# Later LSTM steps by Strassen's seven products, and x through common buffers and DRAM

## The chip, the cores and the metric

The kernel runs on one core of a Trainium2 chip. The metric is the device time of one execution in microseconds (us). The kernel before took 2199.53 us, the median of three runs (2198.49 to 2202.52). The profile shows a further execution, timed at 2196.78 us; its span from the first to the last instruction is 2195.0 us, at a granted TensorE clock of 0.998.

## The reference, cut to what matters

Input x has 128 batches of 64 rows with 256 features, that is 8192 rows. Four layers follow each other, each of the form x = x + f(relu(layernorm(x))):

```python
# layer 0: two graph convolutions with the 64x64 matrix adj, then four LSTMs
h = relu(adj @ (h @ Wg0 + bg0)); h = relu(adj @ (h @ Wg1 + bg1))
for p in range(1, 5):                  # windows of p rows
    nw = 64 // p
    wins = h[:, :nw * p].reshape(128 * nw, p, 256)
    last = lstm(Wih[p-1], Whh[p-1], wins)   # p steps, last hidden state
    h[:, p-1 : nw*p : p] = last
# one LSTM step
g = x_t @ Wih.T + hid @ Whh.T + bias; i, f, gg, o = split(g, 4)
c = sigmoid(f) * c + sigmoid(i) * tanh(gg); hid = sigmoid(o) * tanh(c)
```

Layer 1 mixes with a scaled Laplacian (its largest eigenvalue is needed) and runs four-head attention and a GELU network. Layer 2 is graph attention. Layer 3 projects on the eigenvectors U of a normalised Laplacian made of adj. All is float32.

In the kernel's numbering LSTM 0 has windows of one row, LSTM 1 of two, LSTM 2 of three and LSTM 3 of four. LSTM p has p + 1 steps; step 0 has no hidden state to multiply.

## The kernel before, in words

**Groups.** The 8192 rows are 64 tiles of 128 rows; a group is 8 tiles (16 batches, 1 MB of x). Layer 0 runs on 8 groups, 0 to 7 (`layer0`, L1228). Layers 1 to 3 run on 16 half groups of 4 tiles (`layer1` to `layer3`, groups REST and up). The eigenvectors are computed once (`eig_decomp`, L346, group EIG) by long chains of small operations on DVE, with some on POOL, ACT and TensorE, in the tile arena; part of it copies rows of a matrix through SP's DMA queue.

**Layer 0 of a group.** First a part called the lead (`plan.lead = 1`): layer norm (`ln_stats`, L1178: statistics on DVE, then four small operations on POOL, one of them a power), ReLU on ACT, two graph convolutions. It leaves hT, two tiles of 128 features by 1024 columns; column order is batch row by tile. Two POOL additions with B1T for each half of the tiles end it. Then the LSTMs: LSTM 0 in two halves of 512 columns, LSTM 1 with 512 columns a step, LSTM 2 with 336, LSTM 3 with 256. At the end hT is transposed back and added to x on DVE (L1286).

**An LSTM step** (`lstm_step`, L1196). For each half m of the 256 outputs and each of the gates i, f, g, o: four matmuls of 128 x 128 weights by ncol columns into one PSUM bank (two over the input's feature halves, two over those of the hidden state; step 0 has the first two only). ACT applies sigmoid or tanh with the bias on the way out. DVE updates the cell state cs; ACT takes its tanh; DVE makes the hidden state hs, or in the last step writes into hT.

**x.** Six groups of x stay in SBUF (`places`, NEARLY = 6), loaded between the weights; groups 0 and 1 are put into DRAM after layer 0 and fetched into arena later. Layers 1 to 3 take the groups in the order ORDER, those kept in SBUF first, and hand the room of each x to the common buffers as it ends (`more`).

**Order of the work.** Instructions are recorded first (`Plan.record`), and a planner then writes the order of each engine's queue (`Plan.schedule`, L226). It has a cost for each operation and gives out the common buffers: "big" (4 KB a partition), "mid" (2 KB), "stat", and eight PSUM banks ("bank"). `window` (L967) says how many groups may be under way: in layer 0 the oldest and the next. `reserve` (L970) keeps buffers back for the oldest group. `rank` (L327) chooses among operations that could start: in layer 0 by group (a lead counts as one group earlier), then by the length of the path behind it. Eigenvector work comes last on all engines but TensorE, where it comes first. `burst` (L106) makes one operation of several matmuls. Line numbers in the profile are those of the call that issues the recorded instructions, L343 for nearly all, so groups are told apart by tile names: arena for the eigenvector work, Wih and Whh with big for the LSTMs.

Of the kernel before, what the change touches and what calls it, by code (L numbers as in the profile page):

```python
# [68 lines left out]
class Plan:  # L69
# [6 lines left out]
    def __init__(self, tc, engines, pools, late, reserve, window, aside, ends, slack):  # L76

        self.tc, self.engines, self.pools, self.late = tc, engines, pools, late
        self.reserve, self.window, self.aside, self.ends, self.slack = reserve, window, aside, ends, slack
        self.ops, self.group, self.lead, self.seen = [], 0, 0, {}
        self.run, self.whole = None, False

    def value(self, kind):
        v = Value(kind, self.pools[kind], self.group)  # L90
# [12 lines left out]
        return isinstance(a, Virt) or hasattr(a, "ap")  # L103

    @contextmanager
    def burst(self):  # L106

        self.run, self.whole = None, True
        yield
        self.run.cost = 0.029 * len(self.run.calls)  # L110
        self.run.lat = self.run.cost + 0.22
        self.run.many = True
        self.run, self.whole = None, False

    def record(self, eng, name, args, kw):
        op = self.run
        if op is None:
            op = Op(eng, name, args, kw, self.group)
            op.lead = self.lead
        else:  # L120
            op.calls.append((name, args, kw))
        aps = [(a, i == 0) for i, a in enumerate(args) if self.is_ap(a)]
        aps += [(a, k in ("out", "accum_out")) for k, a in kw.items() if self.is_ap(a)]
        for a, write in aps:
            ap = a.ap if isinstance(a, Virt) else a
            if str(ap.space) == "DRAM" and not self.tc.is_my_tile(ap.tensor):
                continue
            key = ap.tensor.name
            if isinstance(a, Virt):
                key = id(a.val)  # L130
                op.vals[a.val] = True
            step, count = ap.ap[0]
            p0, f0 = (ap.offset // step, ap.offset % step) if step else (0, ap.offset)
            ends = [s * (n - 1) for s, n in ap.ap[1:]]
            region = (p0, p0 + count, f0 + sum(min(e, 0) for e in ends), f0 + sum(max(e, 0) for e in ends) + 1)
            reads, writes = self.seen.setdefault(key, ([], []))
            for log in (reads, writes) if write else (writes,):
                for r, o in log:
                    if o is not op and r[0] < region[1] and region[0] < r[1] and r[2] < region[3] and region[2] < r[3]:
                        op.deps.add(o)  # L140
                        if log is writes:
                            op.late.add(o)
                if write:
                    log[:] = [(r, o) for r, o in log if not (
                        region[0] <= r[0] and r[1] <= region[1] and region[2] <= r[2] and r[3] <= region[3])]
            (writes if write else reads).append((region, op))
        if eng == "PE":

            val = args[0].val
            if val.last and val.last is not op:  # L150
                op.deps.add(val.last)
            val.last = op
        if op is self.run:
            return self.link(op)
        flat = [a.ap if isinstance(a, Virt) else a for a, _ in aps]
        op.cost, op.lat = self.cost(op, flat)

        op.port = eng == "G" or (eng == "V" and not name.startswith("bn_") and "reduce" not in name
                                 and all(str(ap.space) == "SB" for ap in flat))
        op.index = len(self.ops)  # L160
        self.ops.append(op)
        self.link(op)
        if self.whole:
            self.run = op
# [61 lines left out]
    def schedule(self):  # L226
# [20 lines left out]
        while len(order) < len(self.ops):  # L247
            oldest = min(left)
            best = None
            for e, ops in ready.items():  # L250
# [1 line left out]

                runs = sum(op.many and op.ready <= now[e] for op in ops)
                for op in ops:
                    if op.group != self.aside and op.group >= oldest + self.window(oldest):
                        continue
                    t = max(now[e], op.ready, port) if op.port else max(now[e], op.ready)
                    need = {}
# [68 lines left out]
    def rank(self, op):  # L327
        if op.group == self.aside:
            return (-2 if op.eng == "PE" else 1000, op.index)
        if op.eng == "SP":  # L330
            return (op.group, 0, op.index)
        g = min(max(op.group - op.lead, 0), self.ends)
        if op.group < REST:
            return (g, 0, -op.path, op.index)
        return (g, 6 * max(op.group - g, 0) - op.path, op.index)

    def issue(self):
# [549 lines left out]
P = 128  # L887
D = 256
# [1 line left out]
GT = 8  # L890
NG = NT // GT
HT = 4
NEARLY = 6
ORDER = [g % NG for g in range(NG - NEARLY, 2 * NG - NEARLY)]

SETUP, WEIGHTS, ATTN, REST, EIG = -1, NG, NG + 1, NG + 2, 1000
NBIG, NMID, NSTAT, NATTN = 8, 8, 14, 4


class Carver:  # L900
# [33 lines left out]
def gnn_kernel(ctx: ExitStack, tc: tile.TileContext, a, out):  # L934
# [8 lines left out]
    arena = C([P, 10240], "arena")  # L943
    wih = [C([P, 2 * (3 if p == 0 else 4) * D], f"Wih{p}") for p in range(4)]
    whh = [None] + [C([P, 8 * D], f"Whh{p}") for p in range(1, 4)]
    mids = C([P, NMID * 512], "mids")
    pools = {
        "big": [C([P, HT * D], f"big{i}") for i in range(NBIG)],
# [11 lines left out]
            late["big", len(pools["big"])] = groups  # L960
            pools["big"].append(ap[:, i * n:(i + 1) * n])

    more(arena[:, (NG - NEARLY) * GT * D:], (EIG,))
    more(whh[3], tuple(range(NG)))
    more(mids, tuple(range(NG)))

    def window(oldest):  # L967
# [1 line left out]

    def reserve(kind, oldest):  # L970
        if oldest < NG:
            return {"big": 4, "mid": 6, "stat": 1, "attn": 0, "bank": 3}[kind]
        return {"big": 6, "mid": 0, "stat": 2, "attn": 1, "bank": 2}[kind]

    def slack(op):
        if op.eng == "PE":
# [17 lines left out]
    plan.group = SETUP  # L994
    xin = a["x"].rearrange("(g t p) f -> g p t f", p=P, t=GT)
    xout = out.rearrange("(g t p) f -> g p t f", p=P, t=HT)
    places = [C([P, GT * D], f"x{g}") for g in range(NEARLY)]
    X = [places[g % NEARLY].rearrange("p (t f) -> p t f", t=GT) for g in range(NG)]
    for i, g in enumerate(ORDER[:NEARLY]):
        more(places[g % NEARLY], (REST + 2 * i, REST + 2 * i + 1))  # L1000
    dram = ctx.enter_context(tc.tile_pool(name="dram", bufs=1, space=bass.MemoryType.DRAM))
    put = [dram.tile([P, GT, D], F32, name=f"put{g}") for g in range(NG - NEARLY)]
    back = [arena[:, i * GT * D:(i + 1) * GT * D].rearrange("p (t f) -> p t f", t=GT) for i in range(NG - NEARLY)]

    adj2 = C([P, N], "adj2")
    adjT2 = C([P, N], "adjT2")

    for t0, t1 in ((0, 1), (1, 2), (2, 4), (4, 6), (6, 8)):
        ACT.dma_start(X[0][:, t0:t1, :], xin[0][:, t0:t1, :])
    for t, src in ((adjT2, a["adjT"]), (adj2, a["adj"])):  # L1010
        load(t[:N], src)
        load(t[N:], src)
# [7 lines left out]
    for p in range(4):  # L1020
# [5 lines left out]
        else:  # L1026
            load(Wih[p], src)
            load(Whh[p], chunks(a["WhhT"][p]))
        load(X[p + 1], xin[p + 1])
    for g in range(5, NEARLY):  # L1030
        load(X[g], xin[g])

    ident = C([P, P], "ident")
    G.iota(ident, pattern=[[1, P]], base=0, channel_multiplier=-1, allow_small_or_imprecise_dtypes=True)
# [32 lines left out]
    for c in range(2):  # L1067
        V.tensor_scalar(C0T[:, c], row(1), bgc[0][:, c:c + 1], None, op0=ALU.mult)
        for t in range(2):
            V.tensor_scalar(B1T[:, t, c, :], row(0), bgc[1][:, c:c + 1], 1.0 if t else -1.0, op0=ALU.mult, op1=ALU.mult)  # L1070
    G.tensor_tensor(bl, bl, bh, op=ALU.add)
    lapb = C([P, P], "lapb")
    Ub, UTb = C([P, P], "Ub"), C([P, P], "UTb")
    mask1, mask2, ident2, same = (C([P, w], n) for n, w in (("mask1", N), ("mask2", N), ("ident2", N), ("same", P)))
# [150 lines left out]
                o, th = (t.rearrange("p (b w t) -> p b w t", b=2, t=GT) for t in (o, th))  # L1225
            V.tensor_mul(dst, o, th)

    def layer0(x):  # L1228
        plan.lead = 1
        nl = 2 if plan.group == 0 else HT  # L1230
        norms = [ln_stats(x[:, t:t + nl, :], nl) for t in range(0, GT, nl)]
        ayT = [fm() for hf in range(2)]
        for t0 in range(0, GT, nl):
            sc, bi = norms[t0 // nl]
# [2 lines left out]
            for j in range(0, nl, 2):  # L1237
                h.append(two(mid()))
                for t in (j, j + 1):
                    ACT.activation(h[-1][:, t - j, :], x[:, t0 + t, :], AF.Relu, scale=sc(t), bias=bi(t))  # L1240
            ps = mix(lambda t, c: h[t // 2][:, t % 2, tok(c)], lambda t: adjTb, nl)
            for j in range(0, nl, 2):
                ah.append(mid().rearrange("p (c t) -> p c t", c=2))
# [31 lines left out]
        for p in range(1, 4):  # L1275
            k = p + 1
            nw = N // k
            for s in range(k):
                def win(c):
                    return hT[c].rearrange("p (b n t) -> p b n t", b=2, t=GT)[:, :, s:s + (nw - 1) * k + 1:k, :]  # L1280
                ncol = 2 * GT * nw
                lstm_step(p, s, win, hs, cs, ncol, win if s == p else lambda c: hs[:, c, :ncol])
        for t0 in range(0, GT, 2):
            pt = transposes([hT[c].rearrange("p (n t) -> p n t", t=GT)[:, :, t0 + t] for t in range(2) for c in range(2)])
            xt = flat(x[:, t0:t0 + 2, :])
            V.tensor_add(xt, xt, pt)  # L1286

    for g in range(NG):
        plan.group = g
        if g >= NEARLY:  # L1290
            load(X[g], xin[g])
        layer0(X[g])
        if g < len(put):
            SP.dma_start(put[g], X[g])


    plan.group = WEIGHTS
# [218 lines left out]
            ps = proj_tm(lambda c, t: uT[:, t, :], W3b.unsqueeze(1), 1, t0)  # L1516
            V.tensor_add(pair(x, t0), ps, pair(x, t0))

    for i, g in enumerate(ORDER):
        plan.group = REST + 2 * i  # L1520
        x = X[g]
        if g < len(put):
            x = load(back[g], put[g])
        for h in range(GT // HT):
            plan.group = REST + 2 * i + h
            xh = x[:, h * HT:(h + 1) * HT, :]
            layer1(xh)
            layer2(xh)
            layer3(xh)
            for t0 in range(0, HT, 2):  # L1530
                SP.dma_start(xout[g * GT // HT + h][:, t0:t0 + 2, :], xh[:, t0:t0 + 2, :])
    plan.issue()


# [51 lines left out]
```

## Time and profile before

| What | Value |
|---|---|
| Median of three runs | 2199.53 us |
| Span of the profiled execution | 2195.0 us |
| End of layer 0, group 0 / 6 / 7 (last addition to x) | 224 / 1250 / 1404 us |
| End of the eigenvector work on DVE | 1196 us |
| Matmuls in the program | 8002, of which 864 of 512 columns, 608 of 336, 1844 of 256 |
| DVE busy before / after the eigenvector work ends | some 83% of 1200 us / 36 to 38% in the 200 us after |
| DMA | 36.46 MB, mean 17 GB/s, most of it in the first 45 us |

A row of the profile names the engine, the operation, the tile written and the tiles read (buffer numbers left out), shapes and count, then busy time and mean duration. The number of a busy engine counts time in which at least one of its instructions ran. TensorE's weight loads (PEld) run beside its matmuls. In windows, the columns are the window, its length, then busy time and count for PE, PEld, DVE, ACT and POOL, the granted clock, the busy share of the DMA engines, and GB/s.

### The profile page before, as it was taken

To read this page: it belongs to the slowest core of one execution; us is meant where nothing else is said; L and a number is where in the kernel's file an instruction comes from. 1 tells how busy PE (TensorE), PEld (TensorE's weight loads), DVE (VectorE), ACT (ScalarE), POOL (GpSimd) and SP (SyncE) were. 2 spreads that over 40 slices of the span, in tenths; PEclk is the share of its full clock that TensorE was granted. 3 is DMA by queue.
4 is the path that set the end of the run, shared out by engine and by line. 5 is a ranking of instruction groups with operands and counts; after the bars stand their busy time and mean duration, and the time that the engine had idled before them with its cause. 6 is when DMAs were issued, how large, how long until landed. Compare 5 with 4: busy or idle time off the path is not lost.

```text
span 2195.0 us, 41974 instructions
## 1 busy us (share of the span) xinstructions
PE 2164.7 (99%) x15428; PEld 1494.8 (68%) x15428; DVE 1691.9 (77%) x7018; ACT 958.0 (44%) x1937; POOL 569.8 (26%) x856
## 2 busy tenths in 40 slices
PE   8999999999999999999999999999999999999997
PEld 6568468557657747747747757876777777776776
DVE  7768777879999999989885434477877778886797
ACT  2334443333333423323423453445665555545673
POOL 3201111200100000000000114253655465554353
PEclk9999999999999999999999999999999999999999
DMA  7000000010000000000000011000000000000001
GB/s 260 2 2 3 21 2 21 2 39 1 1 1 1 1 1 1 1 1 1 1 5 1 6 42 33 1 1 1 11 11 21 31 11 31 11 11 11 2 1 59
DMA packets 32254, 36.46 MB, mean 17 GB/s; under 512 B 8112, under 2 KB 29488, under 8 KB 31536
## 3 DMA queue, kind: packets, MB, share of 16 engines
q1 hardware_dynamic: 30944, 32.73, 4.6%
q8 instruction: 121, 1.98, 0.4%
q10 hardware_dynamic: 1104, 1.05, 0.2%
q14 instruction: 85, 0.70, 0.1%
HBM read 22.85 MB, written 10.49 MB: 15 GB/s over the span
## 4 chain that ended last, share of the span: by engine, by line
PE 93%; DVE 4%; POOL 1%; ACT 1%; issue 1%; DMA 0%; SPq 0%; DVEq 0%; ACTq 0%; POOLq 0%
PE bank L343 93%; DVE stat L343 1%; DVE x L343 1%; POOL stat L343 1%; DVE big L343 1%; DVE arena L343 1%; DVE mids L343 1%; DVE Whh L343 0%; ACT mids L343 0%; ACT big L343 0%; POOL arena L343 0%; ACT x L343 0%; DMA adj<-in_adj_dram 0%; POOL Whh L343 0%; SPq L343 0%
## 5 line engine op out<-in xcount | busy, mean ns | idle before, releaser
L343 PE MATMUL bank<-big,Wih 128*128 128x256 f32 (+2 forms) x2576 | 854.4, 474 | 1.9 <-DVE big L343 1.4
L343 PEld LDWEIGHTS bank<-big,Wih 128*128 128x128 f32 x2576 | 481.0, 190 | 273.1 <-issue 163.5
L343 ACT ACTIVATE mids<-bank,bl 128x256 f32<-128x256 f32 (+2 forms) x624 | 344.3, 563 | 652.1 <-PE bank L343 648.5
L343 PE MATMUL bank<-big,Whh 128*128 128x256 f32 (+2 forms) x1640 | 506.9, 446 | 0.0
L343 PEld LDWEIGHTS bank<-big,Whh 128*128 128x128 f32 x1640 | 309.6, 190 | 142.1 <-issue 72.2
L343 DVE TENSOR_TENSOR arena<-arena 64x21 f32<-64x21 f32 (+5 forms) x2253 | 358.1, 190 | 33.4 <-POOL arena L343 1.5
L343 POOL TENSOR_SCALAR stat<-stat 128x4 f32<-128x4 f32 (+1 forms) x228 | 69.0, 303 | 831.9 <-DVE stat L343 817.2
L343 DVE TENSOR_TENSOR big<-big,mids 128x256 f32<-128x256 f32 (+2 forms) x192 | 96.9, 505 | 141.5 <-ACT mids L343 139.7
L343 DVE TENSOR_TENSOR big<-mids 128x512 f32<-128x512 f32 (+2 forms) x256 | 146.7, 578 | 64.2 <-ACT mids L343 60.1
L343 DVE SCALAR_TENSOR_TENSOR arena<-arena 64x1 f32<-64x1 f32 (+14 forms) x569 | 119.6, 233 | 16.4 <-POOL arena L343 11.2
L343 POOL TENSOR_TENSOR stat<-stat,mhalf 128x4 f32<-128x4 f32 (+1 forms) x114 | 123.5, 1085 | 6.7
L343 ACT ACTIVATE mids<-big 128x256 f32<-128x256 f32 (+2 forms) x176 | 89.1, 509 | 81.6 <-DVE big L343 56.0
L343 DVE TENSOR_SCALAR arena<-arena 64x1 f32<-64x1 f32 (+9 forms) x535 | 102.7, 200 | 9.2 <-POOL arena L343 0.7
L343 DVE BATCH_NORM_STATS2 stat<-x 128x6 f32<-128x256 f32 x240 | 85.6, 408 | 2.2 <-DMA x<-in_x_dram 2.1
L343 PE MATMUL bank<-Whh,big 128*128 128x256 f32 x336 | 83.8, 383 | 1.4 <-DVE x L343 0.7
L343 POOL MEMSET arena<- 64x2 f32 (+5 forms) x72 | 8.0, 113 | 282.8 <-DVE arena L343 282.8
L343 PEld LDWEIGHTS bank<-Whh,big 128*128 128x128 f32 x336 | 61.4, 190 | 19.3 <-issue 6.7
L343 POOL TENSOR_TENSOR arena<-arena 64x1 f32<-64x1 f32 x66 | 39.6, 599 | 128.3 <-DVE arena L343 65.7
L343 PE MATMUL bank<-Wih,big 128*128 128x256 f32 (+1 forms) x320 | 70.3, 360 | 0.0
L343 ACT ACTIVATE arena<-arena 128x512 f32<-128x512 f32 (+28 forms) x70 | 20.8, 304 | 96.7 <-DVE arena L343 96.3
L343 PE MATMUL bank<-Wg,mids 128*128 128x256 f32 x256 | 61.6, 390 | 0.7 <-ACT mids L343 0.7
L343 POOL TENSOR_TENSOR big<-big,B1T 128x512 f32<-128x512 f32 x32 | 35.8, 1125 | 100.8 <-DVE big L343 54.5
(348 smaller groups left out, 3304.9 us busy)
## 6 DMA issues: line engine op xcount, KB each, us to landing
x<-in_x_dram SPq DMA_DIRECT2D x7, 1024.0 KB, 13.7
out_dram<-x SPq DMA_DIRECT2D x24, 256.0 KB, 2.3
Wih<-in_WihT_dram SPq DMA_DIRECT2D x3, 1024.0 KB, 15.6
Whh<-in_WhhT_dram SPq DMA_DIRECT2D x3, 1024.0 KB, 11.9
put<-x SPq DMA_DIRECT2D x2, 1024.0 KB, 3.9
arena<-put SPq DMA_DIRECT2D x2, 1024.0 KB, 5.6
out_dram<-arena SPq DMA_DIRECT2D x8, 256.0 KB, 2.3
Whh<-in_W_dram SPq DMA_DIRECT2D x2, 512.0 KB, 4.0
```

Source lines behind the costliest of these rows:

```text
L343: getattr(self.engines[op.eng], name)(*map(real, args), **{k: real(a) for k, a in kw.items()})
```

## The change

Steps 1 of LSTM 1, and 1 and 2 of LSTM 2, go through a new function `lstm_fast`. It takes a gate's product W times input as a 2 x 2 block product: the weight's blocks are output halves by feature halves (128 x 128), the input's are feature halves by two halves of the columns (w = ncol / 2: 256 and 168). In place of 8 block products it makes 7, by a form of Strassen's scheme, once with x and once with h, both into the same bank. The sums of weight blocks are made once at the start (`fastw`, POOL, 16 operations of 512 columns, in the new tile sums and partly in place). The sums of input blocks are made in each step by `pieces`: four subtractions on POOL for x, four on DVE for h. A gate uses three banks, a, b and c. Bank a takes product 1, is copied out by ACT, goes on to accumulate product 6 and is copied again, then product 7 and is read by DVE, then product 4. Three DVE additions and the activations (now three for a gate, not two) make the gate out of the banks and the copies. The first six matmuls of a gate are one burst.

x no longer has a place of its own. `fetch` loads halves of a group into big buffers, once for the lead and once more for the addition at the end (held back by `plan.behind` until the last operation recorded before LSTM 3), and every group is put into DRAM, from where layers 1 to 3 fetch it in natural order. There are 12 big buffers in place of 8 and 10 mid in place of 8, and the later room (arena, sums, mids) is given to big. The rank inside layer 0 is now group, then lead first, then program order; SP may work one group further ahead. At the start x of later groups stands behind all weights on SP's queue.

```diff
-        self.run.cost = 0.029 * len(self.run.calls)
+        self.run.cost = cost or 0.029 * len(self.run.calls)
...
-        self.run.many = True
+        self.run.many = cost is None
...
-                    if op.group != self.aside and op.group >= oldest + self.window(oldest):
+                    if op.group != self.aside and op.group >= oldest + self.window(oldest) + (op.eng == "SP"):
...
-            return (g, 0, -op.path, op.index)
+            return (g, -op.lead, op.index)
...
-NBIG, NMID, NSTAT, NATTN = 8, 8, 14, 4
+NBIG, NMID, NSTAT, NATTN = 12, 10, 14, 4
...
+    sums = C([P, 2 * 7 * 4 * P], "sums")
...
-    more(arena[:, (NG - NEARLY) * GT * D:], (EIG,))
+    more(arena, (EIG,))
     more(whh[3], tuple(range(NG)))
+    more(sums, tuple(range(NG)))
...
-            return {"big": 4, "mid": 6, "stat": 1, "attn": 0, "bank": 3}[kind]
-        return {"big": 6, "mid": 0, "stat": 2, "attn": 1, "bank": 2}[kind]
+            return {"big": 7, "mid": 5, "stat": 1, "attn": 0, "bank": 3}[kind]
+        return {"big": 7, "mid": 0, "stat": 2, "attn": 1, "bank": 2}[kind]
...
-        load(X[p + 1], xin[p + 1])
-    for g in range(5, NEARLY):
-        load(X[g], xin[g])
...
+            G.tensor_tensor(s1, a21, a22, op=ALU.add)
+            G.tensor_tensor(s2, s1, a11, op=ALU.subtract)
+            G.tensor_tensor(s3, a11, a21, op=ALU.subtract)
+            G.tensor_tensor(s4, a12, s2, op=ALU.subtract)
+            fastw[p].append({1: a11, 2: a12, 3: s4, 4: a22, 5: s1, 6: s2, 7: s3})
...
+    def pieces(B, eng):
...
+        eng.tensor_tensor(t[0], B(0, 1), B(0, 0), op=ALU.subtract)
+        eng.tensor_tensor(t[1], B(1, 1), t[0], op=ALU.subtract)
+        eng.tensor_tensor(t[2], B(1, 1), B(0, 1), op=ALU.subtract)
+        eng.tensor_tensor(t[3], B(1, 0), t[1], op=ALU.subtract)
+        return {1: B(0, 0), 2: B(1, 0), 3: B(1, 1), 4: t[3], 5: t[0], 6: t[1], 7: t[2]}
...
+        R = [pieces(xs, G), pieces(hs, V)]
+        for nm, q, fn in GATES:
...
+            a, b, c = (bank("gate")[:, :w] for i in range(3))
...
+                for j in range(2):
+                    PE.matmul(ps, L[j][i], R[j][i], start=start and j == 0, stop=j == 1, skip_group_check=True)
...
+            with plan.burst(6 * (0.001672 * w + 0.006)):
+                prod(a, 1, True)
+                prod(c, 2, True)
+                prod(b, 5, True)
+            ACT.copy(p1, a)
+            ACT.copy(g[1][:, w:], b)
+            V.tensor_tensor(g[0][:, :w], c, p1, op=ALU.add)
+            prod(a, 6)
+            ACT.copy(u, a)
+            prod(a, 7)
+            V.tensor_tensor(g[1][:, w:], a, g[1][:, w:], op=ALU.add)
+            prod(a, 4)
+            prod(b, 3)
+            V.tensor_tensor(g[0][:, w:], b, u, op=ALU.add)
+            ACT.activation(g[0], g[0], fn, bias=bias(0))
+            ACT.activation(g[1][:, :w], a, fn, bias=bias(1))
+            ACT.activation(g[1][:, w:], g[1][:, w:], fn, bias=bias(1))
...
+                if s and p in (1, 2):
+                    w = ncol // 2
+                    lstm_fast(p, lambda c, n: win(c)[:, n], lambda c, n: hs[:, c, n * w:(n + 1) * w], cs, w, dst)
+                else:
+                    lstm_step(p, s, win, hs, cs, ncol, dst)
...
+        plan.behind = last
+        x = fetched()
+        plan.behind = None
...
     for g in range(NG):
         plan.group = g
-        if g >= NEARLY:
-            load(X[g], xin[g])
-        layer0(X[g])
-        if g < len(put):
-            SP.dma_start(put[g], X[g])
+        first = [X0] if g == 0 else []
+        x = layer0(lambda: first.pop() if first else [fetch(xin[g][:, i * HT:(i + 1) * HT]) for i in range(2)])
+        for i in range(2):
+            SP.dma_start(put[g][:, i * HT:(i + 1) * HT], x[i])
...
+    for g in range(NT // HT):
+        plan.group = REST + g
+        x = fetch(put[g // 2][:, g % 2 * HT:(g % 2 + 1) * HT])
+        layer1(x)
+        layer2(x)
+        layer3(x)
```

## The prediction

> **What bounds the kernel now.** I read the page from the top: shares of the engines, the chain, the costliest groups; then the busy times in windows of 100 us, and at last the order in time of TensorE.
>
> ```profile
> span 2195.0 us, 41974 instructions
> PE 2164.7 (99%) x15428; PEld 1494.8 (68%) x15428; DVE 1691.9 (77%) x7018; ACT 958.0 (44%) x1937; POOL 569.8 (26%) x856
> PE 93%; DVE 4%; POOL 1%; ACT 1%; issue 1%; DMA 0%; SPq 0%; DVEq 0%; ACTq 0%; POOLq 0%
> ```
>
> The three lines are the span, the busy times and the chain that ended last. TensorE carries 93% of that chain; no other engine has more than 4% of it. A busy PE need not be a full one, so I also looked at how far apart matmuls start, in the timeline:
>
> ```profile
> 641.41 8.94 PE L343 MATMUL bank<-big,Wih 128*128 128x512 f32 x29
> ...
> 1333.82 3.55 PE L343 MATMUL bank<-big,Whh 128*128 128x336 f32 x12
> 1337.21 3.55 PE L343 MATMUL bank<-big,Wih 128*128 128x336 f32 x12
> ...
> 1400.07 1.96 PE L343 MATMUL bank<-ident,big 128*128 128x128 f32 x16
> 1401.86 10.09 PE L343 MATMUL bank<-Wih,big 128*128 128x256 f32 x46
> 1411.88 3.03 PE L343 MATMUL bank<-lapb,arena 64*64 64x64 f32 x192
> ```
>
> Columns: start, duration, group, count. Twelve records of 336 columns start in 1337.21 - 1333.82 = 3.39 us, 0.283 us each; 46 of 256 columns in 10.02 us, 0.218 us, with one change of tile mode in it (0.216 between two neighbours); 16 of 128 in 1.79 us, 0.112; at 512 columns two neighbours are 0.429 us apart. The program has 8002 matmuls and the trace 15428 records: a float32 matmul leaves two records (some are missing). So a matmul costs twice those numbers: 0.859, 0.565, 0.432 and 0.22 us for 512, 336, 256 and 128 columns. Time is proportional to columns, with next to nothing fixed, down to 128: TensorE runs at its rate, and what shortens the kernel is fewer columns.
>
> How much waiting is left? Where two matmuls start farther apart than those pitches, I sum the difference over the trace: 67 us in all, 13 in the first 100 us, 9 from 100 to 1300, 32 from 1300 to 2100, 13 in the last 95. The long middle is almost free of waits. What the other engines have to spare there:
>
> ```profile
> 500.00:600.00 100.00, 100.00 (x636) 74.33 (x635) 92.48 (x466) 37.21 (x79) 5.45 (x9) 1.00 0.01 1
> 800.00:900.00 100.00, 100.00 (x386) 73.14 (x385) 93.81 (x471) 36.04 (x72) 0.00 (x0) 1.00 0.00 1
> 1200.00:1300.00 100.00, 100.00 (x348) 64.51 (x347) 37.85 (x113) 49.31 (x99) 16.83 (x32) 1.00 0.05 15
> ```
>
> Columns: window, its length, busy PE, weight loads, DVE, ACT, POOL. DVE is 92 to 94% busy between 500 and 1100, but mostly with the eigenvector work (tile arena), which the planner gives the lowest rank on DVE; once that has ended (at 1196 us) DVE falls to 38%. The LSTMs alone need about 45 us of DVE in a group of some 170 us.
>
> **What the Trainium skill says.** "TensorE: Matmul & The Clock Gate", section Back-to-back issue gap, gives N/2.4 + 2.5 ns for a warm matmul. With two passes to a record this is 429, 282 and 216 ns for 512, 336 and 256 columns; the trace has 429, 283 and 216, so I use it between two measured widths: 168 columns, 142.5 ns a record, 0.285 us a matmul (an estimate; the straight line from 128 to 256 gives the same). "PSUM — Partial Sum Buffer", The four PSUM rules, allows a synchronised read of a partial sum in the middle of an accumulation group, which the change rests on; no run here shows it yet. "SBUF — State Buffer", Who interferes with whom, says that a DVE operation with two SBUF inputs and a GpSimd one that reads SBUF block each other in full. The trace fits: DVE additions on 256 columns have a median of 424 ns and a mean of 477.
>
> **The change part by part.**
>
> 1. Matmuls. In step 1 of LSTM 1 (512 columns) each of 4 gates x 2 row halves takes 4 matmuls: 32 x 0.859 = 27.5 us a group. After: 7 products x 2 (x and h) x 4 gates = 56 of 256 columns, x 0.432 = 24.2 us. In steps 1 and 2 of LSTM 2 (336 columns): 64 x 0.565 = 36.2 us; after, 112 of 168 columns, x 0.285 = 31.9. Saved: 3.3 + 4.2 = 7.5 us a group, 60 us in 8 groups. The counts of the two programs agree: 256 matmuls of 512 and 512 of 336 columns go, 448 of 256 and 896 of 168 come. If 168 columns cost 0.30 instead, because weight loads (190 ns each by their rows) began to show, 13 us of it would be lost; the 128-column pitch of 0.112 speaks against that.
>
> 2. DVE and ACT. A gate adds 3 DVE additions out of PSUM, 3 ACT copies and one ACT activation; a step adds 4 DVE and 4 POOL subtractions. DVE rows start 0.33 us apart at 256 columns and by their slope about 0.24 at 168: 8 x 16 x 0.33 + 16 x 16 x 0.24 = 104 us more. ACT: copies of 0.374 (256) and some 0.30 (168), 96 + 192 of them, with 96 activations' fixed part about 110 us; ACT is at 36% here, so nothing is on the path for throughput. For DVE I put the order of the new program beside the durations of the old one's rows: groups 1 to 6 need 146 to 156 us of DVE each, with 85 to 94 of eigenvector work, beside 158 to 166 us of TensorE. So DVE stays just below TensorE (93%), and the eigenvector work, which yields, is stretched: its last matmul moves from TensorE's 1174th to its 1284th us of work, near the end of the last LSTM. It is needed by layer 3 and by the buffers in arena, both later, so I cost that at 0, bounds 0 and 10.
>
> 3. New waits inside a gate. Bank a is written, copied by ACT, accumulated into again, copied again, accumulated again. By order, 128 matmuls between 100 and 1300 us of TensorE's work have less than 1.2 us of other matmuls between them and the matmul whose result ACT or DVE has to take first (before: 84). What has to fit in: the end of a matmul (its record is 0.16 us longer than its pitch), 0.30 to 0.37 of copy or 0.41 of addition, three signals. That is 0.65 to 0.8: mostly hidden; I take 0.05 us each on average, 6 us (bounds 0 and, at 0.3 each, 40). Behind a late copy TensorE's whole queue waits, since it runs in order.
>
> 4. The last group. Groups 0 to 6 have the next group's work as filler. Group 7 has none until layer 1 begins. Before, a step's 8 or 16 products with x ran while h was being finished. Now each burst takes x and h together, and h must first go through the four subtractions. From the last product to the next burst: 0.16 + 0.41 addition + 0.69 activation + 1.2 two multiplications + 0.8 two subtractions + signals, about 3.5 us, in three places (into step 1 of LSTM 1, steps 1 and 2 of LSTM 2): 10 us (bounds 3 and 18).
>
> 5. Start. x of group 1 is now issued behind all weights on SP's queue, as the eighth MB where it was the second. At the 350 to 400 GB/s that the windows show from 10 us on, it lands at about 30 us; and POOL's queue has 13 of the 16 weight sums (1.1 to 1.28 us each) ahead of group 1's statistics and most of them ahead of the first additions into hT of group 0. So TensorE loses about 18 us by its 29th us of work, where it lost 14: +4 (bounds 0 and 10).
>
> 6. x through DRAM: 30 fetches of 0.5 MB in place of 7 of 1 MB, 16 puts of 0.5 MB in place of 2 of 1 MB, and 16 fetches in place of 2 for the layers after, spread over windows whose DMA share is 0.00 to 0.17: 0. SP carries the row copies of the eigenvector work too, and one that stands behind a put waits for the put's x; it delays only the eigenvector chain.
>
> 7. Layers 1 to 3. Their matmuls are the same; 36 common buffers in place of 20 plus those that x sets free. Either sign: 0, bounds -8 and +8. ACT has 49 table loads in place of 39 (1.28 us each), beside other work.
>
> Sum on the profile's span: 2195.0 - 60 + 6 + 10 + 4 = 2155 us. The profiled run was timed at 2196.8 and the median of three is 2199.5, 4.5 above the span: 2159.5. The part costs 3 to 5 are skewed, with hidden more likely than stated, so I take 2156.
>
> **The rivals.** (a) All of the saving stays: the waits hide, 2199.5 - 60 + 4 = about 2140 or a little less. For it: the old program keeps TensorE at 9 us of waits in 1200. Against: the last group has no filler. (b) DVE becomes a second bound. At 93% of TensorE's time, with additions blocked by POOL (mean 477 against 424 ns), 5% more for DVE puts it at 98%; then its order, with eigenvector work between, hands lateness on to TensorE: 3 to 5 us a group, 2175 to 2190. (c) Slower: the exchanges of bank a. There are 96 gates with four of them; at 0.16 us lost per exchange, 0.63 a gate, all 60 us are gone, and from 0.7 a gate it is slower, about 2215 at 0.8. For it: a chain of three banks a gate leaves room for two gates in eight banks. Against: by order most exchanges have over 1.6 us of other matmuls between. (d) That 168-column matmuls don't run at the rate is in the bounds of step 1. That fewer products do not appear can be excluded by the counts.
>
> **How the numbers follow.** Forecast (2143 to 2171) 0.64; (a) 0.16; (b) 0.13; (c) 0.06; within 0.2% of 2199.5, about what a measurement can tell from no change, 0.01. So faster 0.93, same 0.01, slower 0.06. The range leaves out the lower half of (a), the upper part of (b) and (c): 2136 to 2184.
>
> **What would show it.** Matmuls of 168 columns at 0.142 us a record and 60 us less of TensorE's work; DVE at 93 to 96% to near the end of the LSTMs; gaps on PE behind ACT copies and DVE additions, 6 us more over groups 0 to 6 and about 10 in group 7; PE waits at the start for POOL or x of 4 us more; the same 45 us of waits from the first layer 1 to the end. Wrong it would be through a DVE that is later than TensorE in every group, or through TensorE waits of over 0.3 us in each gate.

## The result, and the profile after

The changed kernel takes 2166.19 us (median of four runs, 2165.76 to 2169.57), the kernel before 2200.01 us in four runs beside it (2198.49 to 2202.52). The ratio is 0.9849, with a 95% interval of 0.9831 to 0.9866: 33.8 us, or 1.5%, faster. The forecast was 2156 us, 43.5 us faster. So the sign and the range hold, and a fifth of the expected gain is missing.

The head of the page of the kernel after (span, busy time, chain that ended last):

```profile
span 2164.1 us, 45598 instructions
PE 2112.6 (98%) x16580; PEld 1630.7 (75%) x16580; DVE 1800.3 (83%) x7402; ACT 1079.8 (50%) x2331; POOL 653.1 (30%) x968
PE 83%; DVE 11%; POOL 2%; ACT 1%; DMA 1%; issue 1%; SPq 0%; DVEq 0%; ACTq 0%
```

The span fell by 30.9 us. TensorE still carries the chain, but DVE's part of it rose from 4% to 11%, so there may be places where TensorE now waits for DVE. The windows of the kernel after that answer to the three of before show more (columns: window, length, busy PE, weight loads, DVE, ACT, POOL, granted clock, DMA share, GB/s):

```profile
500.00:600.00 100.00, 98.80 (x654) 74.21 (x653) 90.54 (x465) 39.49 (x91) 12.98 (x19) 1.00 0.10 33
800.00:900.00 100.00, 97.07 (x492) 81.90 (x491) 95.00 (x441) 44.42 (x106) 6.46 (x11) 0.98 0.10 32
1200.00:1300.00 100.00, 92.32 (x439) 74.10 (x439) 88.25 (x387) 41.04 (x95) 16.51 (x29) 0.98 0.18 59
```

TensorE was busy for all 100 us of each before. Now up to 8 us are missing, and in two of the three windows the mean granted clock is 0.98.

Was the work saved? Here are two neighbouring groups of matmuls in the timeline of the kernel after (start, duration, group, count):

```profile
647.40 2.44 PE L344 MATMUL bank<-big,sums 128*128 128x168 f32 x16
649.68 0.45 PE L344 MATMUL bank<-big,Whh 128*128 128x168 f32 x2
```

Sixteen records of 168 columns start in 649.68 - 647.40 = 2.28 us, 0.1425 us each, which is the estimated pitch (the distance between the starts of neighbouring matmuls). With the number of records of each width and the pitches, TensorE's work goes from about 2129 to about 2068 us: 60.4 less.

What TensorE loses is the time by which matmuls start farther apart than their pitches. Between the first and the last matmul that is 60.9 us before and 90.2 after. (The 67 us of the prediction count the first and last microseconds too.) In the first 100 us it changed by -0.3 us, from there until group 7 first needs a hidden state by +14.5, in group 7 by +12.2, and after layer 0 by +2.8. What a halved clock costs is in these sums: between 100 and 2100 us there are two stretches of 3.41 us (from 896.7 and 1238.0 us) with a granted clock of 0.50, and half of each, 3.4 us together, is lost. The kernel before has none there. The balance is -60.4 + 29.3 = -31.1, against -30.9 measured. It has to come out, because all that is not work counts as lost; what the sum tells is where.

Where are the 14.5 us? These are the end of group 5 on TensorE and on DVE in the kernel after (in brackets: idle time before the group, and who ended it), the middle of the statistics left out:

```profile
1054.06 4.46 PE L344 MATMUL bank<-big,Wih 128*128 128x512 f32 x10
1060.71 3.67 PE L344 MATMUL bank<-big,Wih 128*128 128x512 f32 x8 [2.19 <-DVE arena L344]
...
1053.39 2.47 DVE L344 TENSOR_TENSOR big<-big,bank 128x512 f32<-128x512 f32 x4
1055.78 0.37 DVE L344 TENSOR_TENSOR arena<-arena 64x21 f32<-64x21 f32 x3
1056.08 0.74 DVE L344 BATCH_NORM_STATS2 stat<-big 128x6 f32<-128x256 f32 x2
...
1059.09 0.29 DVE L344 BATCH_NORM_AGGREGATE stat<-stat 128x2 f32<-128x6 f32 x2
1059.30 1.26 DVE L344 TENSOR_TENSOR big<-mids 128x512 f32<-128x512 f32 x2
```

The same place in the kernel before, the end of its group 4, and the first and the last of DVE's block there:

```profile
904.76 1.92 PE L343 MATMUL bank<-ident,big 128*128 128x128 f32 x16
906.52 8.75 PE L343 MATMUL bank<-big,Wih 128*128 128x512 f32 x20
915.20 1.16 PE L343 MATMUL bank<-adjTb,mids 64*64 64x64 f32 x64
...
906.39 2.48 DVE L343 TENSOR_TENSOR x<-x,bank 128x512 f32<-128x512 f32 x4
911.95 1.34 DVE L343 TENSOR_TENSOR big<-mids 128x512 f32<-128x512 f32 x2
```

At the end of a group DVE does 2.5 us of additions to x, and then the layer-norm statistics of the lead two groups further on. Until that is over, DVE takes no products of the next group's LSTM 0, whose matmuls are TensorE's only filler here (work of the next group that can run while the oldest group waits). The block on DVE is not new: in the kernel before it lasts from 906.39 to 911.95 us, 5.6 us, and in the kernel after 5.9. But before, 20 records of filler (8.75 us) were left for this place. After, 10 are left (4.46 us), and TensorE stands for about 2.2 us, until DVE has gone on to the products at 1059.30. All seven ends of groups 0 to 6 have such a gap (1.3 to 3.1 us beyond the pitch), 12.8 us in all, with 2 to 12 records of filler before it. At five of them the additions and the statistics stand in the way; at the ends of groups 3 and 6 only 2 and 4 records are left, and the additions alone are enough. With 1.7 us of halved clock after the longest gap the ends make 14.5 us, which is the whole difference up to group 7. So next to nothing is left there for the exchanges inside the gates. Group 7 has 9.3 us in gaps of over 0.12 us between 1234 and 1318 us, and 1.7 through the clock.

The busy times by stage, first layer 0 to the last addition to x, then the rest; the first two lines are of the kernel before, the others of the kernel after:

```profile
0.00:1404.00 1404.00, 1395.89 (x7088) 925.61 (x7089) 1077.20 (x5322) 513.29 (x1154) 164.07 (x312) 1.00 0.06 18
1404.00:2195.00 791.00, 768.81 (x8341) 569.19 (x8339) 614.73 (x1697) 444.67 (x783) 405.77 (x544) 1.00 0.05 15
...
0.00:1367.00 1367.00, 1339.99 (x8192) 1058.62 (x8196) 1181.71 (x5706) 617.96 (x1530) 242.78 (x420) 1.00 0.10 32
1367.00:2164.00 797.00, 772.65 (x8404) 572.08 (x8393) 618.61 (x1697) 461.87 (x802) 410.34 (x549) 1.00 0.06 18
```

Layer 0 is 37 us shorter, and the rest 6 us longer. Of the 6 us only 2.8 are waits; 3.4 are matmuls of the later layers that the kernel before had run before its layer 0 ended.

### The profile page after: what moved, and what is told of

Its sections match the earlier page's. It is cut to its first block, busy times and chain, and to the rows that moved or that the text cites. A ratio compares the mean times of both kernels' runs of the same rounds, so it can differ in the third digit from the quotient of the medians.

```text
span 2164.1 us, 45598 instructions
## 1 busy us (share of the span) xinstructions
PE 2112.6 (98%) x16580; PEld 1630.7 (75%) x16580; DVE 1800.3 (83%) x7402; ACT 1079.8 (50%) x2331; POOL 653.1 (30%) x968
## 4 chain that ended last, share of the span: by engine, by line
PE 83%; DVE 11%; POOL 2%; ACT 1%; DMA 1%; issue 1%; SPq 0%; DVEq 0%; ACTq 0%
PE bank L344 83%; DVE arena L344 3%; DVE big L344 3%; DVE stat L344 2%; DVE mids L344 1%; DVE sums L344 1%; POOL stat L344 1%; POOL sums L344 1%; DMA Wih<-in_WihT_dram 1%; ACT mids L344 0%; ACT arena L344 0%; DMA Whh<-in_L_b_dram 0%; DMA big<-put 0%; ACT big L344 0%; SPq L344 0%
## 5 line engine op out<-in xcount | busy, mean ns | idle before, releaser
L344 PE MATMUL bank<-big,Wih 128*128 128x256 f32 (+3 forms) x2400 | 748.2, 435 | 18.7 <-DVE arena L344 9.3
L344 ACT ACTIVATE mids<-bank,bl 128x256 f32<-128x256 f32 (+3 forms) x528 | 275.4, 528 | 407.3 <-PE bank L344 403.5
L344 PE MATMUL bank<-big,Whh 128*128 128x256 f32 (+2 forms) x1624 | 431.0, 368 | 3.5 <-DVE big L344 3.5
L344 PE MATMUL bank<-big,sums 128*128 128x168 f32 (+2 forms) x1728 | 268.8, 307 | 0.0
L344 PEld LDWEIGHTS bank<-big,sums 128*128 128x128 f32 (+1 forms) x1728 | 225.4, 178 | 16.0 <-issue 3.9
L344 ACT COPY mids<-bank 128x168 f32<-128x168 f32 (+2 forms) x393 | 132.1, 357 | 138.1 <-PE bank L344 135.1
L344 ACT ACTIVATE mids<-mids,bl 128x336 f32<-128x336 f32 (+2 forms) x192 | 102.4, 540 | 71.4 <-DVE mids L344 67.6
L344 DVE TENSOR_TENSOR mids<-bank,mids 128x168 f32<-128x168 f32 (+2 forms) x307 | 112.9, 372 | 25.8 <-PE bank L344 22.3
L344 DVE SCALAR_TENSOR_TENSOR arena<-arena 64x1 f32<-64x1 f32 (+15 forms) x565 | 120.9, 237 | 7.5 <-POOL arena L344 3.9
L344 POOL TENSOR_TENSOR big<-big 128x168 f32<-128x168 f32 (+1 forms) x24 | 16.8, 712 | 359.9 <-DVE arena L344 132.2
L344 PEld LDWEIGHTS bank<-Wih,big 128*128 128x128 f32 x512 | 87.7, 190 | 15.4 <-issue 4.5
```

The source lines that it names most:

```text
L344: getattr(self.engines[op.eng], name)(*map(real, args), **{k: real(a) for k, a in kw.items()})
```

## The experiments

The theory was that the missing part is lost at the ends of groups, where the filler is used up too early, and in group 7. The rivals: the x that now goes through DRAM costs it, with the new rank and buffers; the exchanges inside the gates cost it; DVE has become a second bound. The medians of before beside these runs were 2198.05 to 2198.97 us, so I compare ratios; "against after" is the plain difference of the medians.

**Everything but Strassen.** All LSTM steps are computed by eight products; x through DRAM, buffers and rank stay, the sums of weights are not made.

```diff
-    for p in (1, 2):
+    for p in ():
...
-                if s and p in (1, 2):
+                if s and p in ():
```

> All of the change but the seven products: every LSTM step is the old one, the sums of weight blocks are not made, x goes through common buffers and DRAM, the rank and the buffers are those of the changed kernel. Theory (the waits of the changed kernel come with the fast steps, which use up the next group's LSTM 0 as filler and have none in group 7): 2200 to 2209 us, that is the old time with 0 to 6 us from layers 1 to 3, and no gaps of over 1 us on TensorE at the ends of groups 0 to 6. Rival (the gaps at the ends of groups come from x's buffers and the new rank): the same 13 us of gaps at the group ends, 2215 to 2222 us.

Measured: 2201.49 us, ratio 1.0014 [1.0007, 1.0020]. Its windows by stage:

```profile
0.00:1409.00 1409.00, 1398.66 (x7030) 929.13 (x7031) 1073.73 (x5323) 513.60 (x1150) 160.41 (x309) 1.00 0.10 31
1409.00:2201.00 792.00, 772.30 (x8399) 571.35 (x8398) 613.27 (x1696) 446.56 (x788) 409.77 (x548) 0.99 0.06 18
```

They are nearly those of the kernel before, though the DMA moves as much as in the kernel after (31 and 18 GB/s). TensorE loses 67.1 us in it (before: 60.9), and there is no gap over 1 us at the end of a group. So all the rest of the change together costs 2 to 3 us, and on top of it Strassen's steps bring 35 of the 60 us that they save.

**The statistics earlier.** The planner counts a lead as belonging to one group earlier, so that a lead may start before the oldest group ends:

```diff
-                    if op.group != self.aside and op.group >= oldest + self.window(oldest) + (op.eng == "SP"):
+                    if op.group != self.aside and op.group - op.lead >= oldest + self.window(oldest) + (op.eng == "SP"):
```

> The changed kernel, with the lead of a group (layer norm and graph convolutions) let in one group earlier, so that at the end of a group the lead after next can already stand behind it on DVE and be filler for TensorE. Theory (at the end of each of groups 0 to 6 TensorE has no filler while DVE does 4 additions to x and 8 statistics in a row): the seven gaps of 1.3 to 3.1 us (12.8 us together, and some 3 us of halved clock after the longest) go for the most part, 2150 to 2157 us. Rival (DVE as a whole is the bound in layer 0): nothing gained, 2164 to 2172 us, the gaps in other places.

Measured: 2159.84 us, ratio 0.9822 [0.9807, 0.9836], 6.3 us faster than after, and above the expected range. DVE at the end of group 5 in this kernel's timeline, and what TensorE has there after its last transposes:

```profile
1043.76 2.47 DVE L344 TENSOR_TENSOR big<-big,bank 128x512 f32<-128x512 f32 x4
1046.15 0.58 DVE L344 TENSOR_TENSOR arena<-arena 64x21 f32<-64x21 f32 x3
...
1048.63 0.69 DVE L344 TENSOR_TENSOR big<-mids 128x512 f32<-128x512 f32 x1
...
1044.27 31.07 PE L344 MATMUL bank<-big,Wih 128*128 128x512 f32 x72
```

No statistics stand between the additions and the products, and what TensorE loses from 100 us to group 7 falls from 23.2 to 5.9 us. But filler is not short either: 72 records are left, where after has 10. A lead that may start earlier has matmuls of its own, which may have spared those of LSTM 0. So this run does not tell whether the shorter block on DVE or the filler closed the gaps. The whole doesn't gain as much: group 7 has larger gaps (19.5 us against 14.9, one gap of 3.78), and the clock is halved for 6.8 us in it and 3.4 us after it.

**Products with x first.** The burst is split, so that the three products with x, which are ready early, go ahead of those with h:

```diff
-            with plan.burst(6 * (0.001672 * w + 0.006)):
-                prod(a, 1, True)
-                prod(c, 2, True)
-                prod(b, 5, True)
+            for j in range(2):
+                with plan.burst(3 * (0.001672 * w + 0.006)):
+                    for ps, i in ((a, 1), (c, 2), (b, 5)):
+                        PE.matmul(ps, L[j][i], R[j][i], start=j == 0, stop=j == 1, skip_group_check=True)
```

> The changed kernel, with the first three products of a gate split: the three matmuls with x first as one burst, those with h as a second one. Theory (in group 7 TensorE waits at the start of a fast step because the burst of x and h together stands behind the four subtractions of h): the gaps of group 7, 9.3 us together, fall to 4 to 6, total 2159 to 2164 us. Rival (those gaps are exchanges of the banks within a gate): group 7 keeps 8 us or more, total 2164 to 2168 us.

Measured: 2156.82 us, ratio 0.9807 [0.9791, 0.9824], 9.4 us faster than after, more than expected. It was meant for group 7, where the larger gaps fall from 9.3 to between 4 and 5 us. But they also vanish at the ends of groups 0 to 5 (2.66 us remain at that of group 6). Its TensorE timeline at the end of group 5 says why; below it the end of group 4, with DVE's block:

```profile
1036.79 1.50 PE L344 MATMUL bank<-ident,big 128*128 128x128 f32 x12
1038.12 9.61 PE L344 MATMUL bank<-big,Wih 128*128 128x512 f32 x22
1047.66 1.16 PE L344 MATMUL bank<-adjTb,mids 64*64 64x64 f32 x64
...
877.57 8.75 PE L344 MATMUL bank<-big,Wih 128*128 128x512 f32 x20
876.78 2.48 DVE L344 TENSOR_TENSOR big<-big,bank 128x512 f32<-128x512 f32 x4
882.93 0.66 DVE L344 TENSOR_TENSOR big<-mids 128x512 f32<-128x512 f32 x1
```

Twenty-two records of filler are left at the end of group 5, where after has 10 and before 20. DVE's statistics are as late as in the kernel after, and no longer matter: at three of these six ends, that of group 4 among them, all of them stand before the first product. This is what shows the cause: the block is the same, the filler is back, the gaps are gone. The other profiles agree. Apart from the three kernels with the early lead, 17 ends of groups 0 to 5 have 2 to 12 records of filler, and each has a gap of 1.4 to 4.7 us; 36 have 16 to 28 records, and none has a gap over 0.6 us where the filler ends. (At one more, in the kernel before, matmuls of the lead stand there.)

Why the filler lasts is less certain. My reading is that a burst that can't start until h is there lets TensorE take the next group's LSTM 0 in its place, so that at the end of the group it is missing. But the edit also makes each burst half as long for the planner, and shorter bursts in the old order were not tried. (Layer 1 begins worse than in the kernel after: 2.5 us of idle time at 1372 us, then a halved clock.)

**Group 7 by eight products.** Fast steps only in groups 0 to 6 (before group 7, two POOL operations turn an overwritten weight block back):

```diff
-                if s and p in (1, 2):
+                if s and p in (1, 2) and plan.group < NG - 1:
```

> The changed kernel, with the old LSTM steps in group 7 alone (two POOL operations of 512 columns give back the weight blocks that the sums had overwritten). Theory (the fast steps of group 7 lose in waits what they save in columns): TensorE has 7.5 us more of columns and loses 8 to 11 us less in gaps and halved clock, 2161 to 2167 us. Rival (group 7's gaps are not due to its fast steps): all 7.5 us come on top, 2172 to 2175 us.

Measured: 2169.35 us, ratio 0.9866 [0.9851, 0.9881], 3.2 us slower than after, between the two expected ranges. It has 7.5 us more of columns. In its trace group 7 loses 7.4 us in place of 14.9, so the fast steps do cost there about what they save; but after layer 0 it loses 4.0 us more. Its interval overlaps with that of the kernel after, so whether the fast steps pay in group 7 can't be told.

**One LSTM alone.** In place of `(1, 2)`, the tuple is `(1,)` in the one and `(2,)` in the other.

> The changed kernel with the seven products in LSTM 1 alone (8 fast steps of 256 columns, sums made for LSTM 1 alone). Columns saved: 26 us. Theory (what is given back comes with fast steps that need the next group's work as filler, in proportion to their number): a third of the 24 fast steps, so a third of the 26 us given back, about 9: against the kernel without fast steps (2201.5) 17 us less, 2180 to 2190. Rival (the giving back is one fixed cost of group ends, whatever the number of fast steps): most of it stays, 2190 to 2197.

> The changed kernel with the seven products in LSTM 2 alone (16 fast steps of 168 columns). Columns saved: 34 us. Theory: two thirds given back, about 17, and 17 less than 2201.5: 2180 to 2189. Rival (168 columns are short against the exchanges of the banks, so LSTM 2 gains nothing and LSTM 1 all): 2195 to 2202 here and 2170 to 2176 with LSTM 1 alone.

Measured: 2191.03 us (ratio 0.9969 [0.9958, 0.9981]) with LSTM 1 alone, 2186.84 (0.9950 [0.9935, 0.9965]) with LSTM 2 alone. From the 2201.49 of no fast step that is a gain of 10.5 of the 26 us of columns, and of 14.7 of 34; together 25, where both have 35. LSTM 1 alone is in the range of the rival that expected a fixed cost, LSTM 2 alone in that of the theory. The traces fit neither. No group end of the first has a gap over 1 us, and only that of group 6 in the second (2.57 us): the gaps at the ends come when both LSTMs have fast steps, not in proportion to their number. Each alone loses time elsewhere: around group 7 (4.8 us idle at 1336 us in the first; 0.4 to 0.7 us in nearly every gate of group 7 in the second), and after layer 0, where the first loses 42 us and the second 39, against 34 without fast steps and 35 with both. Why layers 1 to 3 begin worse then stays open.

**x subtractions on DVE.** Four subtractions a fast step go from POOL to DVE, 96 in all:

```diff
-        R = [pieces(xs, G), pieces(hs, V)]
+        R = [pieces(xs, V), pieces(hs, V)]
```

> The changed kernel with the four subtractions for x on DVE in place of POOL: about 26 us more of DVE in layer 0 (0.34 us each at 256 columns, 0.24 at 168). Theory (DVE's spare time goes to the eigenvector work, which yields): layer 0 ends within 6 us of the changed kernel's, the eigenvector work 15 to 30 us later, total 2163 to 2174 us, the upper end where its lateness is felt in layers 1 to 3. Rival (DVE is the second bound in layer 0): all of it comes on top, 2184 to 2194 us.

Measured: 2174.79 us, ratio 0.9889 [0.9875, 0.9904], 8.6 us slower than after: just above the range of the theory, and well below the 18 to 28 us that a bound of DVE would have cost. The groups of DVE up to 1330 us, by form, and the windows up to there; in each pair the kernel after stands first:

```profile
L344 DVE TENSOR_TENSOR arena<-arena 64x21 f32<-64x21 f32 x1728 | 239.8, 177 | 16.1
L344 DVE TENSOR_TENSOR arena<-arena 64x21 f32<-64x21 f32 x1728 | 228.1, 171 | 17.1
...
0.00:1330.00 1330.00, 1302.99 (x7861) 1025.59 (x7862) 1159.95 (x5634) 596.12 (x1482) 220.31 (x390) 0.99 0.10 32
0.00:1330.00 1330.00, 1306.42 (x7922) 1026.72 (x7923) 1163.85 (x5759) 598.13 (x1488) 165.40 (x303) 0.99 0.10 32
```

DVE has 96 instructions more, some 26 us by their rows, but is busy only 3.9 us longer (the last column before the clock is POOL, 55 us less): its other operations got shorter when POOL stopped working beside them, as the 64 x 21 additions show. The eigenvector work even ends earlier, at 1310 us. The loss is at the ends of groups once more: five of them have gaps of 1.7 to 4.7 us, behind 2 to 18 records of filler. The longest, 4.5 us idle at 231.6 us, is the end of group 0, where four records are left and DVE is in its additions and statistics from 229.06 to 235.31 us. The clock is halved three times in layer 0, and after it 6.6 us more are lost. That DVE's throughput sets the time is rejected.

**Both mends.** Statistics earlier and products with x first.

> Both changes that gained by themselves: the matmuls with x ahead of those with h, and the lead let in one group earlier. Theory (both fill the same gaps at the ends of groups, so they hardly add): 2153 to 2158 us. Rival (they fill different gaps): 9.4 + 6.3 us less than the changed kernel, 2148 to 2152 us.

Measured: 2149.57 us, ratio 0.9778 [0.9763, 0.9792]: 16.6 us faster than after, and faster than every other version here. I had expected that the two hardly add, since both mend the ends of groups; 6.3 + 9.4 = 15.7, so the totals add in full. Group 7 in this kernel:

```profile
1200.00:1300.00 100.00, 95.44 (x472) 76.07 (x472) 86.92 (x364) 49.63 (x115) 20.71 (x33) 1.00 0.29 86
```

TensorE is busy 95.4 us of this window, against 92.3 after and 100 before. From 100 us to group 7 no gap is over 0.8 us, and between 31 us and the last 10 us the clock is never halved. This is what TensorE loses in each stage, in us, a halved clock included:

| Kernel | From 100 us to group 7 | Group 7 | After layer 0 |
|---|---|---|---|
| Before | 8.7 | 2.7 | 32.5 |
| No Strassen | 8.4 | 5.5 | 33.9 |
| After | 23.2 | 14.9 | 35.3 |
| Statistics earlier | 5.9 | 19.5 | 40.6 |
| Products with x first | 13.4 | 9.0 | 43.6 |
| Both mends | 9.1 | 9.0 | 37.7 |

At the ends of groups the two do not add, just as expected: 17.3 and 9.8 us by themselves, 14.1 together. Group 7 gains from products with x first alone. The totals add because each mend by itself makes the part after layer 0 worse, by 5.3 and 8.3 us, and both together by only 2.4. Why was not tested.

**The old rank.**

```diff
-            return (g, -op.lead, op.index)
+            return (g, 0, -op.path, op.index)
```

> The changed kernel with the old rank inside layer 0 (group, then the length of the path behind the operation). Theory (the gaps at the ends of groups come from the seven products in both LSTMs with x and h in one burst, not from the new rank): gaps of 1 us and more stay at the ends of most groups, 2160 to 2172 us. Rival (the lead-first rank, which puts statistics ahead of the LSTM's multiplications on DVE, makes them): they go, 2150 to 2157 us.

Measured: 2188.91 us, ratio 0.9964 [0.9951, 0.9977], 22.7 us slower than after; neither theory nor rival. I had not thought that the rank matters so much. At the ends of groups the rival was right: 18 to 34 records of filler are left at those of groups 1 to 6, and only that of group 0 has a gap over 1 us (1.59, after 12 records). So the new rank has a part in spending the filler early, beside the fast steps in both LSTMs and the bursts of x and h: without any one of the three most of these gaps are gone. But TensorE loses nearly as much in groups 1 to 6 as in the kernel after (20.7 us from 100 us to group 7), partly in the graph convolutions of the lead (1.88 us idle at 1075 us), and more before and after them: 114.0 us in all, against 90.2. The first 100 us in the kernel after, and then with the old rank:

```profile
0.00:100.00 100.00, 92.89 (x808) 60.43 (x809) 65.75 (x313) 35.83 (x82) 52.09 (x91) 0.97 0.32 111
0.00:100.00 100.00, 89.53 (x779) 57.06 (x779) 62.23 (x303) 31.95 (x74) 50.50 (x91) 0.93 0.32 111
```

Group 0 ends at 237 us, not 227, and layer 0 at 1373, not 1367. The eigenvector work ends at 1390 us, after layer 0, and the rest takes 815 us, not 797. So 6 us are lost in layer 0 and 18 in the layers after.

**All three.** Both mends, and the x subtractions on DVE.

> The fastest so far (matmuls with x first, lead one group earlier), with the four subtractions for x on DVE in place of POOL, since in the kernel with that change alone DVE was busy only 4 us longer up to 1330 us. Theory (POOL's subtractions block DVE for about as long as DVE needs to do them itself): the same time as without, 2147 to 2155 us. Rival (DVE now bounds layer 0): 2158 us and more.

Measured: 2153.38 us, ratio 0.9795 [0.9778, 0.9811]. That is in the range of the theory. Its interval meets that of both mends, so whether it matters here which engine subtracts is within what can't be told.

## Why the prediction was right, and what it missed

*Step 1, the columns (-60):* right, -60.4, at the estimated pitch. The formula that the estimate used gives the measured pitches if its fixed 2.5 ns is counted once in a record and the columns twice; with both twice it would be 432, 285 and 218 ns.

*Step 2, DVE and ACT:* Over the span DVE is busy 108 us longer (104 predicted), ACT 122 (110). The eigenvector work is stretched as foreseen, from 1196 to 1336 us. Its price of 0 was not isolated, and step 7 touches it.

*Step 3, exchanges inside a gate (+6):* about 0, since the ends of groups alone make up what groups 0 to 6 lost more. Rival (c) is far off. That the exchanges hide is seen in the 168-column rows of the kernel after, by form (after the second bar: idle time before the group, and who ended it):

```profile
L344 PE MATMUL bank<-big,sums 128*128 128x168 f32 x896 | 151.6, 306 | 0.0
L344 PE MATMUL bank<-big,Whh 128*128 128x168 f32 x512 | 114.9, 307 | 0.7 <-DVE big L344 0.7
L344 PE MATMUL bank<-big,Wih 128*128 128x168 f32 x384 | 86.5, 307 | 2.2 <-DVE mids L344 1.7 <-DVE arena L344 0.4
```

Before 1792 records 2.9 us are idle.

*Step 4, group 7 (+10):* 12.2, of which 9.3 us in the larger gaps and 1.7 through the halved clock. The place was right, and the cause fits: products with x first take 5.9 us of it away, eight products there 7.5.

*Step 5, the start (+4):* TensorE loses the same in the first 100 us (17.1 and 16.8), so 0.

*Step 6, x through DRAM (0):* right; with buffers and rank, 2 to 3 us.

*Step 7, layers 1 to 3 (0, bounds -8 and +8):* +6 in length, inside the bounds, of which 2.8 are waits. The kernels with fast steps and the new rank have 795 to 802 us here, the one without fast steps 792. Why stays open. The old rank, where the eigenvector work ends after layer 0, has 815; that fits a wait for it, but was not tested.

*The step that failed* is the opening of step 4, "Groups 0 to 6 have the next group's work as filler." At the ends of groups it had been used up: 12.8 us of gaps and 1.7 of halved clock that the sum doesn't have. Steps 3 and 5 were 6 and 4 us too dear and hid most of it, by luck: 14.5 - 6 - 4 leaves 4.5 of the 9 us between the sum (2155) and the span (2164.1), and steps 4 and 7 make the rest with 2 and 3 us more than predicted. I had noted that a burst takes x and h together, but costed that only where there is no filler. Where there is some, the burst does not wait; it seems to spend the filler early. Rival (a) was wrong for this reason, and rival (b), DVE as a second bound with 3 to 5 us a group, in its mechanism: DVE did hand lateness on, 1.3 to 3.1 us a group, but by a block of work that was there before the change, and more filler took the gaps away without less work for DVE. Its argument from additions that POOL blocks was weak for most of layer 0: in the kernel before, additions and products on 256 columns take 418 ns in the mean from 100 to 1300 us; the mean of 477 comes from later ones.

## What to carry to other kernels

Fewer columns pay in full only where something else is left to cover each boundary: after such a change, count the filler that remains at the end of a stage, not only the load of the engines in its middle. Give an operation that takes two operands its early operand first, or it will spend what you need later. When two mends act on the same gaps, still run both together, and then look where the gain is: here the totals added, but at the boundary itself the gains did not. And a gap can have several causes at once: here each of several edits by itself closed most of those at the ends of groups.

## What the runs showed of the hardware

*A short gap can cost more than half as much again.* "TensorE: Matmul & The Clock Gate", section What's actually happening, of the Trainium skill says that TensorE falls to half its clock after an idle window of about 3.4 us. Here shorter gaps were enough. The kernel after, right after its gaps at 892.5 and 1235.0 us, and the matmuls that follow the second:

```profile
1237.51 0.78 PE L344 MATMUL bank<-big,Whh 128*128 128x256 f32 x2 [2.48 <-DVE big L344]
...
896.70:900.10 3.40, 3.40 (x5) 1.35 (x4) 3.16 (x13) 1.16 (x3) 3.15 (x7) 0.50 0.01 3
1238.00:1241.40 3.40, 3.40 (x9) 2.72 (x9) 2.99 (x17) 0.37 (x1) 1.76 (x5) 0.50 0.00 0
```

Over all profiles of this case, between 100 and 2100 us, 14 idle times on TensorE are of 2.4 us or more, and after 13 of them the clock was halved, for 3.41 or 6.83 us. Of 13 between 1.9 and 2.4 us, 7 were followed by it. The limit is not sharp: in the kernel with the old rank 1.88 us of idle time were followed by it too. So here a gap of about 2 us or more could cost up to 1.7 or 3.4 us more than its own length.

*POOL's work slows DVE's even when neither waits for the other by a semaphore.* 26 us of subtractions moved from POOL to DVE cost DVE 3.9 us of busy time up to 1330 us, as shown above. In the pair of kernels with both mends it was 9.9 us. In both pairs the mean of the 64 x 21 additions fell from 177 to 171 ns.
